# Sixteen-head attentions: normalising after a transpose to query rows, and adding the residual for four entries at once

## The chip, the cores and the metric

The kernel runs on one core of one Trainium2 chip. The metric is the device time of one execution, in microseconds (us). Before the change three executions took 15986.45, 16016.19 and 16036.29 us; the median is **16016.19 us**. The profiled execution has a span of 16008.8 us.

## What is computed

The reference is a decoder of four layers over 32 entries of 128 tokens with 128 features, in 32-bit floats. The state x is updated by twelve blocks in turn, each in the form

```
x = x + block(layernorm(x))
```

Five of the twelve blocks are attentions with 16 heads of 8 features, and they are what this change touches: L0 attention (causal), L0 cross attention, L1 attention, L1 cross attention (with a mask given as input) and L2 cross attention. For one entry they compute

```
q, k, v = projections of layernorm(x)   # cross attentions: k and v from a context of 128 tokens
scores  = q_h k_h^T / sqrt(8)           # for each head h, 128 x 128
attn    = softmax(scores)               # over the keys
out_h   = attn v_h                      # 128 x 8 for each head
x       = x + concat(out_h) Wo + bo     # L1 attention has no Wo; L0 attention has no bo
```

The softmax is computed as exp(scores) without taking off a maximum. Its denominator, the sum of the exponentials over the keys, is divided out after the product with v. Since no maximum is taken off, the kernel keeps the extremes of all reciprocals of these sums; if one lay out of bounds at the end, the whole program would be run again in a general form. With the inputs used here that second run does not happen.

## The kernel before

Class `Fast` holds the attention as `mha`, called once for each of the five blocks. It loops over 8 groups (`b4`) of 4 entries, 40 groups over the five blocks. The state X lies in SBUF for the whole program, with the 128 tokens of an entry on the 128 partitions.

**Head of a group.** `norm4` normalises four entries on VectorE (L333), `trans4` transposes them on TensorE (L341) into one PSUM tile and copies it to SBUF on VectorE (L343) as xnT. TensorE then makes q, k and v (through the helper `mm`, so that all these matmuls are recorded as L315). ScalarE and VectorE write q out as four masked copies `qTm` (L1385 to L1391), ScalarE writes kT and the values `va` (L1405). In `va` each head has its 8 value columns in one of four places of a row of 64, and eight columns of ones in the matching place of the second half.

**Loop over entries.** For each of four entries (`j2` and `jj`) TensorE makes the scores of 16 heads in PSUM tiles `sc`, transposed: keys on partitions, queries along the free dimension. In the causal block (L0 attention) and the one with a mask (L1 cross attention) a matmul with the tile `drop` comes first. ScalarE takes the exponential into `PT` (L1424). Then the matmuls `av` add up, for each head, its 8 outputs and eight copies of its sum. The PSUM tile `av` of two entries has queries along the free dimension; on partitions, for t = 0 and 1, it has 32 rows of outputs (four heads of 8) and 32 rows with the sums that belong to them.

**Normalising.** For two entries together VectorE takes, in four pieces of 32 partitions, the reciprocal of the sums (L1436, tile `rc`, 32x256) and multiplies the outputs with it (L1437, into `oT`). Since heads and features are on the partitions of `oT`, each sum has to be inverted eight times, once for each feature. `look` then reduces `rc` to its minimum and maximum (L1306).

**Projection and residual.** `oT[:, j, :]` has the layout that a matmul takes as stationary operand, so `y` of one entry is one matmul with Wo (in L1 attention one transpose, L1444), with a second one of one row for the bias in the cross attentions (`brow`). `addx` adds y to X (L347) and takes the statistics for the next layernorm (`stats`, L320 and L321), one entry at a time.

What sets the order: each engine works through its own queue. The order in these queues is chosen when the program is built, by a scheduler that takes ready instructions by their order in the source; the instructions wait for each other by semaphores. The buffers count too: all PSUM tiles made by `p1` (`p`, `av`, `y`) share four slots of one bank each, those made by `p2` (`sc`) two slots of two banks each. SBUF tiles of the loop (`wk`) have two slots each.

Of the kernel before, what the change touches and what calls it, by code (L numbers as in the profile page):

```python
# [13 lines left out]
F32 = mybir.dt.float32  # L14
# [4 lines left out]
ALU = mybir.AluOpType  # L19
# [1269 lines left out]
class Fast(General):  # L1289
# [38 lines left out]
    def mha(self, pre, cross, scale, causal=False, mask=None, out=True):  # L1328
        if self.general:
            return super().mha(pre, cross, scale, causal, mask, out)  # L1330
        nc, tc = self.nc, self.tc
        ob = f"{pre}_bo" in self.row_at
        with ExitStack() as es:
            wk = es.enter_context(tc.tile_pool(name=pre, bufs=2))
# [25 lines left out]
            if cross:  # L1360
# [12 lines left out]
            for b4 in range(NB // 4):  # L1373
                xnT = self.trans4(wk, self.norm4(wk, self.X, b4))
                kvT = self.ctxT[:, 512 * b4:512 * b4 + 512] if cross else xnT
                qp = self.p1([128, 512])
                self.mm(qp, self.mat(f"{pre}_q"), xnT)

                qTm = wk.tile([128, 4, 4, 128], F32, tag="qTm", name="qTm")
                for r in range(4):  # L1380
                    o = qTm[:, r].rearrange("p b q -> p (b q)")
                    m = self.sm("m4")[:, r:r + 1]
                    if r < 2:
                        if cross:
                            nc.scalar.activation(o, qp, AF.Identity, bias=qb[:, r:r + 1], scale=m)  # L1385
                        else:
                            nc.scalar.activation(o, qp, AF.Copy, scale=m)
                    elif cross:
                        nc.vector.tensor_scalar(o, qp, m, qb[:, r:r + 1], ALU.mult, ALU.add)
                    else:  # L1390
                        nc.vector.tensor_scalar(o, qp, m, None, ALU.mult)  # L1391
                kp = self.p1([128, 512])
                self.mm(kp, self.mat(f"{pre}_k"), kvT)
                kT = wk.tile([128, 512], F32, tag="kT", name="kT")
                if cross:
                    nc.scalar.activation(kT, kp, AF.Identity, bias=self.col(f"{pre}_bk"))
                else:
                    nc.scalar.copy(kT, kp)
                vp = self.p1([128, 512])
                for j in range(4):  # L1400
                    c = slice(128 * j, 128 * j + 128)
                    self.mm(vp[:, c], kvT[:, c], self.mat(f"{pre}_v"))
                va = va2[b4 % 2]
                diag = bass.AP(va.tensor, va.offset, [list(va.ap[0]), [256, 16], [72, 4], [1, 8]])
                nc.scalar.copy(diag, vp.rearrange("p (g r e) -> p g r e", g=16, r=4))  # L1405
                oT = wk.tile([128, 4, 128], F32, tag="oT", name="oT")
                rc = wk.tile([128, 4, 128], F32, tag="rc", name="rc")
                for j2 in range(2):

                    av = self.p1([128, 2, 2, 128], "av")  # L1410
                    for jj in range(2):
                        j = 2 * j2 + jj
                        c = slice(128 * j, 128 * j + 128)
                        PT = wk.tile([128, 16, 128], F32, tag="PT", name="PT")
                        for s in range(2):
                            sc = self.p2([128, 2, 512], "sc")
                            if drop is not None:
                                for u in range(2):
                                    self.mm(sc[:, u, :], self.identh[:, 0, :], drop.rearrange("p r q -> p (r q)"),
                                            stop=False)  # L1420
# [12 lines left out]
                    for s in range(2):  # L1433
                        for t in range(2):
                            g = 32 * (2 * s + t)
                            nc.vector.reciprocal(rc[g:g + 32, b2, :], av[64 * t + 32:64 * t + 64, s])  # L1436
                            nc.vector.tensor_tensor(oT[g:g + 32, b2, :], av[64 * t:64 * t + 32, s],  # L1437
                                                    rc[g:g + 32, b2, :], ALU.mult)
                self.look(rc)
                for j in range(4):  # L1440
                    b = 4 * b4 + j
                    y = self.p1([128, 128], "y")
                    if not out:
                        nc.tensor.transpose(y, oT[:, j, :], self.ident)  # L1444
                    else:
                        self.mm(y, oT[:, j, :], self.mat(f"{pre}_o"), stop=not cross)
                        if cross:
                            self.mm(y, self.ones, brow, start=False)
                    self.addx(b, y)


STAGES = ("l0_attn", "l0_xattn", "l0_ffn", "l1_attn", "l1_xattn", "l1_ffn", "l2_attn", "l2_xattn", "l2_ffn",
# [31 lines left out]
```

## Time and profile before

| what | value |
|---|---|
| TensorE (PE) busy | 9793.1 us, 61% of the span |
| VectorE (DVE) busy | 6850.5 us, 43% |
| ScalarE (ACT) busy | 3482.7 us, 22% |
| GpSimd (POOL) busy | 2735.0 us, 17% |
| reductions of L1306, 80 | 682 ns each |
| multiplies of L1437, 320 | 417 ns each |
| residual adds X<-X,y of L347 in the first 4160 us, 192 | 293 ns each |
| exponentials of L1424, 320 | 1022 ns each |
| mean clock granted to TensorE | 0.732 |

The five attentions lie in the first quarter of the span: 39 to 347, 347 to 705, 1345 to 1680, 1680 to 2012 and 3807 to 4156 us. The rest of the program (feed-forward blocks, other attentions and a six-layer local-attention stack that begins near 8600 us) does not call the changed function.

How to read the profile: a row of the groups has the line, the engine, the operation, the tiles as out<-in, the shapes (partitions x elements) and the count; then, after a bar, the busy time in us and the mean of one in ns; then the idle time of that engine just before, with what ended most of it. A row of the timeline has the start and the duration in us, then the same names, and in brackets the idle time before it and its releaser. PE is TensorE's matmul, PEld its load of the stationary operand. A 32-bit matmul is recorded as two passes, so one `y` is two rows in a count. A row of busy times by stretch gives the stretch, its length, the busy time (and instructions) of PE, PEld, DVE, ACT and POOL, then TensorE's granted clock as a share of full speed, the DMA share and GB/s.

### The profile page before, as it was taken

How to read it: one execution, taken by the hardware profiler on the slowest of the kernel's cores; microseconds unless marked ns; L12 is line 12 of the kernel's file. 1: busy time of each engine (PE TensorE's matmuls, PEld its weight loads, DVE VectorE, ACT ScalarE, POOL GpSimd, SP SyncE). 2: the span in 40 equal slices, each digit the busy share in tenths (PEclk: the TensorE clock that was granted, in tenths of full speed). 3: DMA queues.
4: the chain of work that ended last, by engine and by line, in shares of the span. 5: the costliest groups of instructions: out<-in, count | busy, mean ns of one | idle time of the engine just before them, and what ended most of it. 6: DMA issues, size and time to landing. Idle time of an engine off the chain costs nothing.

```text
span 16008.8 us, 131017 instructions
## 1 busy us (share of the span) xinstructions
PE 9793.1 (61%) x51289; PEld 6778.4 (42%) x51289; DVE 6850.5 (43%) x16132; ACT 3482.7 (22%) x4582; POOL 2735.0 (17%) x1578
## 2 busy tenths in 40 slices
PE   6676744447754444344445667667667667767667
PEld 3453333335433322233223445445445444544544
DVE  5545521124333333433334444444444444444444
ACT  2212200011101111111111333333333333333332
POOL 0000055530000000000000221221221221221221
PEclk8756856656666666666666888888888888888888
DMA  0000000001000010000100000000000000000000
GB/s 19 1 0 1 1 30 26 24 20 44 1 11 17 17 22 17 17 17 17 21 18 19 1 1 7 1 1 7 1 1 7 1 1 7 1 1 1 1 1 6
DMA packets 151407, 160.46 MB, mean 10 GB/s; under 512 B 18562, under 2 KB 130915, under 8 KB 145406
## 3 DMA queue, kind: packets, MB, share of 16 engines
q1 hardware_dynamic: 125340, 115.11, 3.3%
q0 software_dynamic: 24576, 33.60, 0.7%
q8 instruction: 410, 6.72, 0.2%
q10 hardware_dynamic: 866, 3.26, 0.1%
q14 instruction: 215, 1.76, 0.0%
HBM read 114.94 MB, written 36.96 MB: 9 GB/s over the span
## 4 chain that ended last, share of the span: by engine, by line
PE 34%; DVE 18%; POOL 7%; ACT 6%; DMA 4%; issue 2%; SPq 0%; ACTq 0%; POOLq 0%; DVEq 0%
PE av L315 6%; PE y L315 4%; PE op L315 4%; DMA rows<-scr 3%; DVE work L1050 3%; PE qk L315 3%; PE p L1200 3%; POOL raw L1183 3%; PE pt L1227 2%; DVE raw L1181 2%; DVE rt L1178 2%; POOL raw L1193 2%; DVE thr L1052 2%; PE sc L315 2%; PE tp L315 2%
## 5 line engine op out<-in xcount | busy, mean ns | idle before, releaser
L1183 POOL TENSOR_TENSOR raw<-raw,rt 128x1024 f32<-128x1024 f32 x384 | 902.2, 2349 | 5399.9 <-DVE raw L1181 5351.9
L315 PE MATMUL av<-va,PT 128*128 128x65 f32 x6144 | 1019.0, 318 | 346.8 <-ACT PT L1229 346.7
L315 PEld LDWEIGHTS av<-va,PT 128*128 128x128 f32 x6144 | 902.0, 226 | 662.9 <-ACT PT L1229 662.9
L315 PE MATMUL tp<-mix,ex 128*128 128x128 f32 (+1 forms) x2048 | 302.0, 315 | 1358.5 <-POOL ex L1063 1358.5
L315 PE MATMUL qk<-wqkv,zs 128*128 128x512 f32 x1536 | 847.4, 669 | 439.8 <-DVE raw L1181 269.6
L1200 PE MATMUL p<-ident,raw 128*128 128x128 f32 x3072 | 525.9, 344 | 597.2 <-POOL raw L1193 597.2
L315 PEld LDWEIGHTS tp<-mix,ex 128*128 128x128 f32 (+1 forms) x2048 | 254.2, 173 | 1401.4 <-POOL ex L1063 1362.9
L1436 DVE RECIPROCAL rc<-av 32x256 f32<-32x256 f32 x320 | 561.9, 1756 | 521.1 <-PE av L315 517.8
L1200 PEld LDWEIGHTS p<-ident,raw 128*128 128x128 f32 x3072 | 480.5, 183 | 669.5 <-POOL raw L1193 669.5
L1178 DVE TENSOR_TENSOR rt<-qk,tab 128x512 f32<-128x512 f32 x768 | 498.6, 686 | 555.4 <-ACT sq L1174 290.6
L1193 POOL TENSOR_TENSOR raw<-raw,ss 128x2048 f32<-128x2048 f32 x192 | 690.7, 3618 | 118.2 <-DVE ss L564 118.2
L1234 DVE RECIPROCAL rs<-av 128x4 f32<-128x4 f32 x768 | 140.3, 183 | 1327.1 <-PE av L315 1327.1
L1229 ACT COPY PT<-pt 128x512 f32<-128x512 f32 x768 | 449.9, 586 | 941.5 <-PE pt L1227 941.5
L315 PE MATMUL mp<-rows,mix 128*128 128x512 f32 (+1 forms) x320 | 191.9, 766 | 733.9 <-DMA rows<-scr 733.9
L1174 ACT ACTIVATE sq<-qk 128x1024 f32<-128x1024 f32 x384 | 393.3, 1024 | 1130.6 <-DVE ss L1184 756.3
L315 PE MATMUL vp<-wqkv,zs 128*128 128x512 f32 x768 | 418.6, 672 | 330.4 <-DVE t L1222 167.8
L1227 PE MATMUL pt<-ident,t 128*128 128x128 f32 x3072 | 536.6, 303 | 137.2 <-ACT t L1223 137.2
L315 PEld LDWEIGHTS qk<-wqkv,zs 128*128 128x128 f32 x1536 | 273.4, 203 | 731.1 <-issue 579.6
L1201 DVE COPY qkT<-p 128x512 f32<-128x512 f32 x384 | 265.6, 692 | 716.7 <-PE p L1200 716.7
L1059 POOL TENSOR_TENSOR ex<-ex,e 128x1188 f32<-128x1188 f32 x32 | 85.9, 2683 | 2762.6 <-DVE e L1058 2697.7
L605 POOL DMA_INDIRECT gd<-in_tdn,idx x512 | 483.1, 943 | 432.0 <-DVE idx L598 181.7
L1223 ACT ACTIVATE t<-t 128x1024 f32<-128x1024 f32 x384 | 407.8, 1062 | 650.9 <-DVE t L1222 650.2
(364 smaller groups left out, 20372.4 us busy)
## 6 DMA issues: line engine op xcount, KB each, us to landing
scr<-dots SPq DMA_DIRECT2D x32, 1056.0 KB
rows<-scr SPq DMA_DIRECT2D x512, 66.0 KB
T<-flt SPq DMA_DIRECT2D x16, 1024.0 KB
wqkv<-in_dqkv SPq DMA_DIRECT2D x6, 1536.0 KB
gd<-in_tdn,idx POOLq DMA_INDIRECT x512
gt<-in_tup,idx POOLq DMA_INDIRECT x256
wo<-in_dwo SPq DMA_DIRECT2D x6, 512.0 KB
X<-in_x SPq DMA_DIRECT2D x4, 512.0 KB
```

What stands on the lines that cost most here:

```text
L315: self.nc.tensor.matmul(out, lhsT=lhsT, rhs=rhs, start=start, stop=stop)
L605: self.nc.gpsimd.indirect_dma_start(out=out, out_offset=None, in_=table, in_offset=bass.IndirectOffsetOnAxis(ap=idx, axis=0))
L1050: nc.vector.match_replace(out=work[:, 0:n], in_to_replace=m8, in_values=cur, imm_value=-3.4e38)
L1174: nc.scalar.activation(sq, pp, AF.Square)
L1178: nc.vector.tensor_tensor(t[:, :, o:o + 32], pp[:, :, n:n + 32], tab[:, w, 1, o:o + 32].unsqueeze(1).to_broadcast([128, 16, 32]), ALU.mult)
L1183: nc.gpsimd.tensor_tensor(r, r, t, ALU.add)
L1193: nc.gpsimd.tensor_tensor(raw, raw, rn.unsqueeze(2).to_broadcast([128, 32, 64]), ALU.mult)
L1200: nc.tensor.transpose(p[:, c, :], flat[:, o:o + 128], self.ident)
L1223: nc.scalar.activation(t, t, AF.Exp, scale=8.0)
L1227: nc.tensor.transpose(pt[:, c, :], t[:, 4 * e + c, :], self.ident)
L1229: nc.scalar.copy(PT, pt)
L1436: nc.vector.reciprocal(rc[g:g + 32, b2, :], av[64 * t + 32:64 * t + 64, s])
```

## The change

The normalising is moved to the other side of a transpose. ScalarE copies `av` of two entries out of PSUM into `avs`; four transposes on TensorE bring it to query rows (`tp`: queries on 128 partitions, outputs and sums along the free dimension). There a sum is needed once for a head and a query, so VectorE's reciprocal covers 32 elements on 128 partitions (two entries of 16 heads), and the multiply, with the reciprocal broadcast over the eight features, 256 elements on 128 partitions. The result `ao` has query rows, so that L1 attention, which has no projection, can add it to X as it is; the others transpose it back with `trans4` (four transposes and a copy on VectorE) for the projection. The tile `y` holds all four entries in one PSUM bank, and one add of 128x512 takes the place of four of 128x128; the statistics are taken after it. `look` reduces 64 elements in place of 512.

```diff
--- before.py
+++ after.py
@@ -1403,8 +1403,8 @@
                 va = va2[b4 % 2]
                 diag = bass.AP(va.tensor, va.offset, [list(va.ap[0]), [256, 16], [72, 4], [1, 8]])
                 nc.scalar.copy(diag, vp.rearrange("p (g r e) -> p g r e", g=16, r=4))
-                oT = wk.tile([128, 4, 128], F32, tag="oT", name="oT")
-                rc = wk.tile([128, 4, 128], F32, tag="rc", name="rc")
+                ao = wk.tile([128, 4, 16, 8], F32, tag="ao", name="ao")
+                rc = wk.tile([128, 4, 4, 4], F32, tag="rc", name="rc")
                 for j2 in range(2):
 
                     av = self.p1([128, 2, 2, 128], "av")
@@ -1429,24 +1429,34 @@
                                     h = 4 * (2 * s + t) + r
                                     self.mm(av[64 * t:64 * t + 64, s, jj, :], va[:, j, h, :], PT[:, h, :],
                                             start=r == 0, stop=r == 3)
+                    avs = wk.tile([128, 2, 2, 128], F32, tag="avs", name="avs")
+                    nc.scalar.copy(avs, av)
+
+                    tp = self.p1([128, 2, 2, 2, 2, 4, 8], "tp")
+                    for jj in range(2):
+                        for s in range(2):
+                            nc.tensor.transpose(tp[:, jj, s].rearrange("p t w r e -> p (t w r e)"), avs[:, s, jj, :],
+                                                self.ident)
+                    tv = tp.rearrange("p j s t w r e -> p (j s t) w r e")
                     b2 = slice(2 * j2, 2 * j2 + 2)
-                    for s in range(2):
-                        for t in range(2):
-                            g = 32 * (2 * s + t)
-                            nc.vector.reciprocal(rc[g:g + 32, b2, :], av[64 * t + 32:64 * t + 64, s])
-                            nc.vector.tensor_tensor(oT[g:g + 32, b2, :], av[64 * t:64 * t + 32, s],
-                                                    rc[g:g + 32, b2, :], ALU.mult)
-                self.look(rc)
-                for j in range(4):
-                    b = 4 * b4 + j
-                    y = self.p1([128, 128], "y")
-                    if not out:
-                        nc.tensor.transpose(y, oT[:, j, :], self.ident)
-                    else:
-                        self.mm(y, oT[:, j, :], self.mat(f"{pre}_o"), stop=not cross)
+                    rv = rc[:, b2].rearrange("p j g r -> p (j g) r")
+                    nc.vector.reciprocal(rv, tv[:, :, 1, :, 0])
+                    nc.vector.tensor_tensor(ao[:, b2].rearrange("p j (g r) e -> p (j g) r e", g=4), tv[:, :, 0],
+                                            rv.unsqueeze(3).to_broadcast([128, 8, 4, 8]), ALU.mult)
+                self.look(rc.rearrange("p j g r -> p j (g r)"))
+                if out:
+                    oT = self.trans4(wk, ao.rearrange("p j h e -> p j (h e)"), "oT")
+                    y = self.p1([128, 4, 128], "y")
+                    for j in range(4):
+                        self.mm(y[:, j, :], oT[:, 128 * j:128 * j + 128], self.mat(f"{pre}_o"), stop=not cross)
                         if cross:
-                            self.mm(y, self.ones, brow, start=False)
-                    self.addx(b, y)
+                            self.mm(y[:, j, :], self.ones, brow, start=False)
+                else:
+                    y = ao.rearrange("p j h e -> p j (h e)")
+                x = self.X[:, 4 * b4:4 * b4 + 4, :]
+                nc.vector.tensor_tensor(x, x, y, ALU.add)
+                for j in range(4):
+                    self.stats(x[:, j, :], 4 * b4 + j)
 
 
 STAGES = ("l0_attn", "l0_xattn", "l0_ffn", "l1_attn", "l1_xattn", "l1_ffn", "l2_attn", "l2_xattn", "l2_ffn",
```

More of the change, by code (lines that the diff above doesn't have):

```diff
@@ L1439, in mha @@
-                self.look(rc)
-                for j in range(4):
-                    b = 4 * b4 + j
-                    y = self.p1([128, 128], "y")
-                    if not out:
-                        nc.tensor.transpose(y, oT[:, j, :], self.ident)
-                    else:
-                        self.mm(y, oT[:, j, :], self.mat(f"{pre}_o"), stop=not cross)
-                        if cross:
-                            self.mm(y, self.ones, brow, start=False)
-                    self.addx(b, y)
+                    avs = wk.tile([128, 2, 2, 128], F32, tag="avs", name="avs")
@@ new lines, in mha @@
+                    rv = rc[:, b2].rearrange("p j g r -> p (j g) r")
[8 more added lines that the diff above has]
+                        self.mm(y[:, j, :], oT[:, 128 * j:128 * j + 128], self.mat(f"{pre}_o"), stop=not cross)
+                        if cross:
+                            self.mm(y[:, j, :], self.ones, brow, start=False)
+                else:
+                    y = ao.rearrange("p j h e -> p j (h e)")
```

## Prediction

> **What bounds the kernel now.** I read the page first, then the groups of VectorE by line, then the timeline over one group of four entries in each of the five attentions, and last the busy times of single groups. Of the 16008.8 us the five attentions hold the stretches 39 to 347, 347 to 705, 1345 to 1680, 1680 to 2012 and 3807 to 4156 us, 1682 us in all (the five windows' sum); the change can act only there. The page shows the row that it removes:
>
> ```profile
> L1436 DVE RECIPROCAL rc<-av 32x256 f32<-32x256 f32 x320 | 561.9, 1756 | 521.1 <-PE av L315 517.8
> ```
>
> The mean of one is 1756 ns, and there are eight in each of the 40 groups. What counts is where they lie. The timeline of the sixth group of the L0 cross attention:
>
> ```profile
> 603.08 1.09 PE L315 MATMUL av<-PT,va 128*64 128x128 f32 x16
> ...
> 604.22 1.75 DVE L1436 RECIPROCAL rc<-av 32x256 f32<-32x256 f32 x1 [1.61 <-PE av L315]
> ...
> 606.63 1.76 DVE L1436 RECIPROCAL rc<-av 32x256 f32<-32x256 f32 x1
> ...
> 609.18 1.75 DVE L1436 RECIPROCAL rc<-av 32x256 f32<-32x256 f32 x1
> ...
> 611.92 1.76 DVE L1436 RECIPROCAL rc<-av 32x256 f32<-32x256 f32 x1
> ...
> 614.52 0.50 PEld L315 LDWEIGHTS y<-mats,oT 128*128 128x128 f32 x2 [9.29 <-DVE oT L1437]
> 614.52 0.80 PE L315 MATMUL y<-mats,oT 128*128 128x128 f32 x2 [9.10 <-DVE oT L1437]
> ...
> 617.41 0.71 PEld L341 LDWEIGHTS p<-ident,xn 128*128 128x128 f32 x4 [0.22 <-issue]
> ```
>
> The last av matmuls end at 604.17. TensorE's next work but for the tail of entry 0's and 1's projections is at 614.52, 10.35 us later, and the next group's first transposes (617.41) stand behind the projections. The four reciprocals of the second pair of entries lie wholly on that path; those of the first pair (593.73 to 602.6) lie beside the scores of entries 2 and 3 and cost nothing. So a group is a chain: head (transposes, q, k, v) 7.3 us, loop over four entries (scores 582.80 to av's end 604.17) 21.4, wait 10.35, projections 2.9: 41.9 us, the spacing of the undisturbed groups.
>
> The busy times of two such groups show a second limit, TensorE's clock (the column behind POOL):
>
> ```profile
> 478.50:527.70 49.20, 35.44 (x194) 20.75 (x192) 24.82 (x39) 10.47 (x12) 0.00 (x0) 0.60 0.00 1
> 573.20:615.10 41.90, 27.09 (x193) 15.96 (x192) 24.76 (x39) 10.47 (x12) 0.00 (x0) 0.79 0.00 1
> ```
>
> Same instructions, 0.60 instead of 0.79, 7.3 us longer. Within a group q/k matmuls of the head take about 0.85 us, and the projections are spaced 0.73 us apart after the wait but 0.42 us inside the loop: the wait puts TensorE at half clock, and the head pays.
>
> **What the Trainium skill says.** "TensorE: Matmul & The Clock Gate", section "Part 1: The HAM clock gate (the "warmup" mystery)", says that the clock is halved after an idle window of about 3.4 us and restored after a busy one; the trace agrees in kind (10 us of wait, then 0.73 for 0.42 us). The same page, "Part 4: PE-mode transpose", says that transposes do not count as busy in the same way; the trace before does not separate this, so I count the new transposes as no help for the clock. "VectorE: DVE Perf Modes", section "Why `tensor_reduce` can't reduce along partition axis", says that the engine streams along the free dimension and that each partition is a lane of its own, so 32 rows should cost what 128 do. The trace agrees: L1437's multiply of 32x256 takes 417 ns, L1235's of 128x256 takes 424.
>
> **The change, part by part.** Per group of four entries.
>
> VectorE loses 8 reciprocals x 1756 = 14.0 us and 8 multiplies x 417 = 3.3. It gets 2 reciprocals of 128x32 (353 ns, L326's row of just that shape) and 2 multiplies of 128x256 (424): 1.6 us. The two reductions of L1306 go from 512 elements (682 ns) to 64; those of L1313 and L1314, of 40 elements, take 162 and 187, so I estimate 215 each. Four residual adds of 0.29 become one of 128x512, about 0.68 (L658, same shape, one input in PSUM); the statistics stay. With an output projection, one copy of 128x512 comes in (0.69, L343). VectorE falls from 24.8 to about 9 us per group and is no bound at all.
>
> ScalarE gets 2 copies of 128x512 out of PSUM, 0.585 each (L1405). It is busy 10.5 of 41.9 us, so the sum costs nothing; the second copy is on the path.
>
> TensorE gets 8 transposes of av, and 4 of ao with a projection; 4 transposes go in l1_attn. Four in a row take 1.06 to 1.11 us after a wait (L341); warm I estimate 0.85 (0.21 between starts in L1261's runs, plus the end). The first pair's four add 0.85 us to the loop; entries 0 and 1's projections, two in L0a and two with bias in the cross attentions, leave it, but only one of them (0.42) stood between av matmuls.
>
> The new path from the end of av to the projection: semaphore 0.2, copy 0.58, 0.2, transposes 0.85, 0.2, reciprocal 0.35, multiply 0.47, 0.2, transposes of ao 1.0, 0.2, copy 0.66, 0.2: **5.1 us in place of 9.7 to 10.35**. The two reductions run beside the second transposes. The 0.2 is what stands between an end and a dependent start on another engine (0.21 before L347 and L343). But now all four projections are behind it: with bias eight pairs of passes at 0.73 = 5.8 us against 2.9; without bias four at 0.5 = 2.0 against 1.0.
>
> The next group's transposes were always behind the last y (617.41 after 616.69), and y still takes its PSUM slot first, so I keep that order. Queued behind them on VectorE: the joined add (0.68) and up to eight statistics operations (4 x 0.47) can stand before the copy of xnT, for which q, k and v wait. In before the add was 0.29 and the copy came at once. I charge 0.8 us with a projection, 2.6 us in l1_attn, where no projection lies between.
>
> Sums at the clock of now: l0_attn loop 20.9 - 0.42 + 0.85 = 21.3, path 5.1, y 2.0, head 6.85 + 0.8: 36.0 against 38.4, 2.4 saved. Cross: 21.4 + 0.43 + 5.1 + 5.8 + 8.1 = 40.8 against 41.9, 1.1 saved; the masked one is 40.2 against 41.3, the same. l1_attn: loop 21.2 - 0.3 + 0.85 = 21.75, copy and transposes 1.9, head 7.3 + 2.6 = 9.9: 33.5 against 38.7, 5.2 saved. Eight groups each: (2.4 + 3 x 1.1 + 5.2) x 8 = **87 us**.
>
> The clock: the wait without TensorE work shrinks from 10 us to three gaps of about 1 us. It will still fall to half somewhere in them, but the 5.8 us of projections and the transposes after them then run without a gap, so it should be back by q, k and v. In the cross attentions the last third of the projections (8 x 0.31 saved at most = 2.5; I take 1.0) and most of four q/k passes at 0.85 and the v passes (about 4.5 us at half; I take 2.0 saved): 3.0. l0_attn has 2.0 us of projections: 0.8. l1_attn has two gaps of about 1 us and less: 1.2. Together (3 x 3.0 + 0.8 + 1.2) x 8 = **88 us**. Forecast 16016 - 175 = **15841 us**.
>
> **Rivals.** (a) The clock stays as now: the chain shrinks, the half clock covers tail and head alike. For it: the path holds transposes and one short burst. 16016 - 87 = 15929. (b) More than forecast: also the disturbed loops disappear. Mean spacing of groups is 44.2, 41.7 and 43.8 us in l0_xattn, l1_attn and l2_xattn against 41.9, 38.7 and 41.9 undisturbed: (2.3 + 3.0 + 1.9) x 8 = 58 us; and without the charge for the queue (0.8 x 4 + 2.6) x 8 = 46: 15737. Against it: these drops come in the middle of the loop (L1a, 1531 to 1545 us), where the change adds little. (c) A new wait eats it: the first pair's transposes wait for ScalarE's copy, which stands behind two exponentials (1.94 us together), with all later scores queued behind them on TensorE. Twice per group, 80 x 1.94 = 155 us: 15996, no change. Against it: av ended at 593.7, the exponentials began at 594.83, so the copy (0.58) fits ahead of them. (d) Slower: transposes in the loop lower TensorE's activity, and the three attentions without mask matmuls run their loops at half clock. The group at 0.60 took 49.2; 24 groups going from a mean of 43.2 to 48.2 cost 120 us, and at a clock of 0.5, by the same slope (7.3 us per 0.19), 3.8 us more each, 211 in all; less 87: 16049 to 16140, middle 16095. For it: these loops already drop by themselves. Against it: 0.85 us of transposes in 21 us is little.
>
> **How the numbers follow.** Forecast 0.45, (a) 0.25, (b) 0.15, (c) 0.08, (d) 0.07. The bound of 0.3% is 48 us: faster below 15968, slower above 16064. Forecast, (a) and (b) are faster, 0.85; (c) and a part of (d) no change, 0.09; the rest slower, 0.06. The range goes from a little below (b) to just past (a), 15700 to 15970, which leaves out (c), (d) and the tail of (b).
>
> **What would show it.** Right, if the reciprocal's row shrinks to 80 of about 353 ns, TensorE's wait before the projections splits into three of about 1 us, and the head's q/k passes fall from 0.85 toward 0.5 us. Rival (a) if they stay at 0.85; (c) if the transposes of av wait on ScalarE in the loop; (d) if groups in l0_xattn show a clock near 0.6. Wrong altogether if the next group's transposes move ahead of the projections: then the path is hidden too, and the time falls below 15700. Work outside the five attentions should keep its time; should it not, the forecast fails for a reason not treated here.

## The result, and the profile after

Four executions of the changed kernel took 15756.74 to 15808.76 us, median **15768.08 us**, against 16016.68 us for the kernel before on the same chip: ratio **0.9851, 95% interval 0.9828 to 0.9874**. The forecast was 15841 us. The profiled spans are 16008.8 and 15754.9 us.

The time went where the prediction looked for it. From the first `rstd` to the last residual add of each attention, read from the two traces:

| attention | before, us | after, us | gained | forecast | spacing of groups before | after |
|---|---|---|---|---|---|---|
| L0 self (causal) | 317.0 | 273.5 | 43.5 | 25.6 | 38.6 | 32.8 |
| L0 cross | 355.3 | 309.0 | 46.3 | 32.8 | 44.5 | 38.5 |
| L1 self | 336.8 | 268.3 | 68.5 | 51.2 | 41.0 | 31.5 |
| L1 cross (masked) | 334.2 | 306.9 | 27.3 | 32.8 | 41.4 | 37.7 |
| L2 cross | 351.7 | 300.1 | 51.6 | 32.8 | 44.0 | 37.2 |

The five sum to 237 us; the rest of the program took 14313.8 us before and 14297.2 after. "Spacing" is the mean of the seven distances between the first writes of `qTm` of successive groups.

The page and the groups by shape of the changed kernel, as they answer to the reciprocal's row of before:

```profile
PE 9835.9 (62%) x51705; PEld 6797.8 (43%) x51705; DVE 6166.0 (39%) x15564; ACT 3530.6 (22%) x4662; POOL 2735.4 (17%) x1578
L1443 DVE RECIPROCAL rc<-tp 128x32 f32<-128x32 f32 x80 | 32.4, 405 | 902.7 <-PE tp L1438 902.7
```

The reciprocals fell from 561.9 us to 32.4. Their median is 358 ns, as the prediction took; one took 2321 ns and lifts the mean to 405. VectorE as a whole lost 684 us, and the program only 254: most of VectorE's work had lain beside other work.

The same place in the timeline as shown of before, in the second half of a group of the L0 cross attention:

```profile
527.21 0.59 ACT L1433 COPY avs<-av 128x512 f32<-128x512 f32 x1 [1.19 <-PE av L315]
527.85 0.66 PE L1438 MATMUL tp<-ident,avs 128*128 128x128 f32 x4 [0.69 <-ACT avs L1433]
528.34 0.38 PE L341 MATMUL p<-ident,ao 128*128 128x128 f32 x2
528.54 0.36 DVE L1443 RECIPROCAL rc<-tp 128x32 f32<-128x32 f32 x1 [8.91 <-PE tp L1438]
528.94 0.42 DVE L1444 TENSOR_TENSOR ao<-tp,rc 128x256 f32<-128x256 f32 x1
...
529.42 0.44 PE L341 MATMUL p<-ident,ao 128*128 128x128 f32 x2 [0.69 <-DVE ao L1444]
529.89 0.69 DVE L343 COPY oT<-p 128x512 f32<-128x512 f32 x1 [0.28 <-PE p L341]
530.64 0.80 PE L315 MATMUL y<-mats,oT 128*128 128x128 f32 x2 [0.78 <-DVE oT L343]
531.37 0.79 PE L315 MATMUL y<-brow,ones 1*128 1x128 f32 x2
...
536.43 1.11 PE L341 MATMUL p<-ident,xn 128*128 128x128 f32 x4
536.53 0.69 DVE L1457 TENSOR_TENSOR X<-X,y 128x512 f32<-128x512 f32 x1 [5.95 <-PE y L315]
537.58 0.69 DVE L343 COPY xnT<-p 128x512 f32<-128x512 f32 x1 [0.36 <-PE p L341]
...
538.32 2.08 PE L315 MATMUL p<-xnT,mats 128*128 128x512 f32 x2 [0.78 <-DVE xnT L343]
```

TensorE's one wait of 10.35 us is now three of 0.69, 0.69 and 0.78 us, 3.47 us with the work between them. Behind it the four projections run without a gap for 5.79 us. And yet the pairs of passes in them start 0.73 us apart (530.64 to 531.37), as before behind the long wait, and the two passes for q that follow take 2.08 us, where in the L0 self attention the four for q and k together take 1.98 (from 202.47).

The busy times of these stretches show it (after the busy counts: the clock). First the path, the projections with bias and the head in the L0 cross attention; then the same three in the L0 self attention; then one loop over four entries in each:

```profile
527.17:530.64 3.47, 1.31 (x9) 0.84 (x9) 1.72 (x5) 0.59 (x1) 0.00 (x0) 0.94 0.00 0
530.64:536.43 5.79, 5.79 (x17) 4.00 (x17) 0.00 (x0) 0.00 (x0) 0.00 (x0) 0.50 0.00 0
536.43:543.75 7.32, 6.54 (x18) 3.85 (x17) 4.03 (x12) 2.13 (x3) 0.00 (x0) 0.50 0.00 0
...
196.46:199.93 3.47, 2.00 (x12) 0.98 (x11) 1.73 (x5) 0.59 (x1) 0.00 (x0) 1.00 0.00 0
199.93:200.93 1.00, 1.00 (x9) 1.00 (x9) 0.00 (x0) 0.00 (x0) 0.00 (x0) 1.00 0.00 0
200.93:206.49 5.56, 3.47 (x18) 2.12 (x17) 4.76 (x16) 2.33 (x4) 0.00 (x0) 1.00 0.00 0
...
543.75:564.71 20.96, 17.45 (x165) 9.67 (x164) 0.78 (x2) 9.03 (x10) 0.00 (x0) 1.00 0.00 1
174.05:196.46 22.41, 21.25 (x178) 10.71 (x179) 0.78 (x2) 8.67 (x9) 0.00 (x0) 1.00 0.00 1
```

In the cross attention everything behind the path runs at 0.50, although TensorE is busy for 12.33 of these 13.11 us. In the self attention, which has no bias, the clock stays full. The last two rows are used below: with mask matmuls (174.05) TensorE is busy 0.95 of the loop, without (543.75) 0.83, and the loop with them is 1.45 us longer.

For comparison the last projections (two of four) and the head before the change, in the group that the prediction shows:

```profile
614.52:617.41 2.89, 2.89 (x8) 2.00 (x8) 2.11 (x6) 0.00 (x0) 0.00 (x0) 0.50 0.00 0
617.41:624.70 7.29, 6.32 (x21) 3.69 (x22) 2.99 (x6) 2.40 (x4) 0.00 (x0) 0.56 0.00 0
```

The head takes 7.32 us where it took 7.29: in the cross attention the shorter wait has not brought the clock back. The clock records change at steps of 3.41 us. In the group of the changed kernel they are at half from 530.25 to 543.90 us, four steps. This is the second of them:

```profile
533.66:537.08 3.42, 3.42 (x11) 2.52 (x12) 0.55 (x1) 0.00 (x0) 0.00 (x0) 0.50 0.00 0
```

TensorE was never idle in it, with projections and bias passes, and the clock stayed at half after it.

### The profile page after: what moved, and what is told of

Its sections match the earlier page's. It is cut to its first block, busy times and chain, and to the rows that moved or that the text cites. A ratio compares the mean times of both kernels' runs of the same rounds, so it can differ in the third digit from the quotient of the medians.

```text
span 15754.9 us, 131362 instructions
## 1 busy us (share of the span) xinstructions
PE 9835.9 (62%) x51705; PEld 6797.8 (43%) x51705; DVE 6166.0 (39%) x15564; ACT 3530.6 (22%) x4662; POOL 2735.4 (17%) x1578
## 3 DMA queue, kind: packets, MB, share of 16 engines
q10 hardware_dynamic: 866, 3.26, 0.1%
## 4 chain that ended last, share of the span: by engine, by line
PE 35%; DVE 19%; POOL 7%; ACT 6%; DMA 4%; issue 2%; SPq 0%; ACTq 0%; POOLq 0%; DVEq 0%
PE av L315 6%; PE y L315 4%; PE op L315 4%; DMA rows<-scr 3%; DVE work L1050 3%; PE qk L315 3%; PE p L1200 3%; POOL raw L1183 3%; PE pt L1227 2%; DVE raw L1181 2%; DVE rt L1178 2%; POOL raw L1193 2%; DVE thr L1052 2%; PE sc L315 2%; PE tp L315 2%
## 5 line engine op out<-in xcount | busy, mean ns | idle before, releaser
L315 PE MATMUL sc<-qTm,kT 32*128 32x512 f32 x1536 | 511.7, 717 | 77.4 <-DVE P L518 63.3
```

The lines of the kernel that those rows point to most:

```text
L315: self.nc.tensor.matmul(out, lhsT=lhsT, rhs=rhs, start=start, stop=stop)
```

## The experiments

Twelve kernels ran, in four sets. Each set has its own runs of the kernel before, on its own chip; the kernel before differs by up to 1% between chips, so only ratios are compared. A block is an attention from its first `rstd` to its last residual add. Mean spacing of groups, from the traces (us):

| kernel | ratio, 95% | L0 self | L0 cross | L1 self | L1 cross | L2 cross |
|---|---|---|---|---|---|---|
| before | 1 | 38.6 | 44.5 | 41.0 | 41.4 | 44.0 |
| the change | 0.9851 (0.9828–0.9874) | 32.8 | 38.5 | 31.5 | 37.7 | 37.2 |
| e1_norm | 0.9861 (0.9845–0.9878) | 34.5 | 38.4 | 30.9 | 37.4 | 39.8 |
| e2_resid | 1.0055 (1.0038–1.0072) | 36.3 | 45.7 | 42.2 | 37.8 | 45.7 |
| e2b_nohoist | 0.9999 (0.9990–1.0008) | 39.5 | 43.5 | 40.9 | 41.3 | 43.2 |
| e3_nobias | 0.9855 (0.9835–0.9874) | 33.0 | 36.9 | 31.5 | 33.7 | 40.6 |
| e4_hold_before | 1.0002 (0.9993–1.0011) | 38.6 | 43.1 | 39.9 | 41.2 | 43.7 |
| e4c_hold36 | 0.9976 (0.9964–0.9988) | 38.7 | 42.0 | 39.9 | 39.3 | 42.7 |
| e5_biasfirst | 0.9870 (0.9852–0.9887) | 33.3 | 37.8 | 31.5 | 31.6 | 41.9 |
| e7_zeromask | 0.9857 (0.9839–0.9875) | 33.4 | 37.3 | 31.5 | 37.5 | 37.7 |
| e10_zero_bias | 0.9779 (0.9762–0.9797) | 33.5 | 31.8 | 31.5 | 31.6 | 31.6 |
| e12_fullrow | 0.9886 (0.9869–0.9902) | 32.8 | 42.3 | 33.2 | 36.6 | 38.3 |
| e13_fullrow_zero | 0.9837 (0.9821–0.9853) | 32.6 | 36.6 | 31.5 | 36.6 | 37.0 |
| e11_pipe_zero_bias | 0.9743 (0.9726–0.9759) | 28.9 | 30.7 | 26.2 | 29.9 | 30.4 |

### Which half of the change carries the gain

**The normalising alone** (`e1_norm`): the changed kernel with a projection tile and an add for each entry, as before.

```diff
-                    y = self.p1([128, 4, 128], "y")
-                    ...
-                nc.vector.tensor_tensor(x, x, y, ALU.add)
+                    y = self.p1([128, 128], "y")
+                    self.mm(y, oT[:, 128 * j:128 * j + 128], self.mat(f"{pre}_o"), stop=not cross)
+                    ...
+                    self.addx(b, y)
```

> The normalising on query rows alone; projections, residual adds and statistics stay one entry at a time, as before. Theory 1 (the shorter path from av to the projections, and the clock that follows from it, are the whole gain): about 15770 us, within 40 us of the changed kernel, and next group's transposes still behind the four projections. Rival 2 (the joined y tile and the single add carry a good part of it): 15850 us or more.

0.9861 against 0.9851: the intervals overlap, as theory 1 has it, so the normalising carries all that can be measured.

**The joined residual alone** (`e2_resid`): the kernel before with `y` of four entries in one tile and one add.

```diff
-                    y = self.p1([128, 128], "y")
...
-                    self.addx(b, y)
+                y = self.p1([128, 4, 128], "y")
...
+                x = self.X[:, 4 * b4:4 * b4 + 4, :]
+                nc.vector.tensor_tensor(x, x, y, ALU.add)
```

> The joined y tile and the single residual add alone, on top of the kernel before; the reciprocals stay on 32 rows. By the prediction's own steps it can only lose: the projections of entries 0 and 1 wait with the others, (1.0 + 3 x 2.9 + 0.3) x 8 = 80 us, so about 16095 us. Rival 3 (one y tile takes one PSUM slot instead of four, so the next group's transposes, q, k and v no longer stand behind the projections of entries 2 and 3 and fill the 10 us wait): up to 7.3 us for each of 35 group boundaries, 255 us, so 15760 to 15900 us; q and k matmuls would then lie between the reciprocals in the trace.

It costs 0.55% (77 us between the medians). That this is close to the 80 us of the first theory is luck: the projections of entries 0 and 1 do not wait (in the group below they start at 513.97 and 515.82 us, before the wait). Rival 3 had the new order right and its effect wrong. With one PSUM slot for four projections in place of four, the next group's transposes, q, k and v move ahead of the projections of entries 2 and 3. The timeline of a group of the L0 cross attention in this kernel shows what that does:

```profile
517.35 0.69 DVE L343 COPY xnT<-p 128x512 f32<-128x512 f32 x1
...
521.08 1.75 DVE L1436 RECIPROCAL rc<-av 32x256 f32<-32x256 f32 x1
...
522.87 0.81 DVE L1389 TENSOR_SCALAR qTm<-p,c_small,qb 128x512 f32<-128x512 f32 x1
...
524.12 1.76 DVE L1436 RECIPROCAL rc<-av 32x256 f32<-32x256 f32 x1
525.92 0.81 DVE L1389 TENSOR_SCALAR qTm<-p,c_small,qb 128x512 f32<-128x512 f32 x1
...
526.78 2.07 PE L315 MATMUL sc<-qTm,kT 32*128 32x512 f32 x2 [3.21 <-DVE qTm L1389]
...
528.78 0.80 PE L315 MATMUL y<-mats,oT 128*128 128x128 f32 x2
```

The head now lies in the wait, but its writes of `qTm` stand between reciprocals of 1.75 us in VectorE's queue, so the next scores wait 3.21 us for them. That alone is not the loss. The two attentions with mask matmuls became shorter with the same reciprocals in the queue, L0 self from 317.0 to 311.7 us and L1 cross from 334.2 to 318.6. The three without became 26 to 30 us longer each, and there the time at half clock grew, in the L0 cross block from 185 to 279 us.

**The same without the new order** (`e2b_nohoist`): `e2_resid` with three one-column matmuls that take the PSUM slots that the four tiles took, so the order stays that of before.

```diff
+                    if j:
+                        d = self.p1([128, 1], "d")
+                        self.mm(d, oT[:, j, :], self.ident[:, 0:1])
```

> The same as the residual part alone, but entries 1, 2 and 3 each also take a PSUM slot for a matmul of one column whose result nobody reads, so that four slots are taken in a group as before. Rival 3: the next group's transposes are behind the projections again and the gain of the residual part is gone, 16000 to 16100 us. If the gain were VectorE's (one add in place of four), this kernel would be as fast as the residual part alone.

0.9999: with the order kept the loss is gone. The single add is worth nothing here; what cost was the head moved ahead, in the three attentions whose loops then ran at half clock.

### Is it the path or the clock

**Without bias** (`e3_nobias`): the changed kernel without the bias matmuls in the three cross attentions, which leaves the bias out.

```diff
-                        if cross:
-                            self.mm(y[:, j, :], self.ones, brow, start=False)
```

> The changed kernel with the bias of the output projection left out in the three cross attentions (four one-row matmuls per group). Theory 4 (TensorE falls to half clock there because the projections with their one-row bias matmuls keep it too little occupied): the clock stays full from group to group as in L0 attention, a cross group goes from 37.5 to about 30.5 us, 24 groups, 168 us: about 15600 us. Rival 5 (the clock falls in the gaps of the path from av to the projections, whatever follows): only the time of the bias matmuls goes, 3.8 us per group, 91 us: about 15675 us, and the clock of a cross group stays near 0.8.

Neither number came: 0.9855, where the change has 0.9851. The masked attention gained (37.7 to 33.7), but groups of the other two lay at 30 to 33 or at 41 to 48: many lost inside the loop, at half clock, what they had gained on the path. This gave the next theory: a loop without mask matmuls lies at the edge of what keeps the clock up.

**Clock held, chain unchanged** (`e4_hold_before`, `e4c_hold36`): the kernel before with unread matmuls in its wait, 24 and then 36.

```diff
+                    if j == 2:
+                        hd = self.p2([128, 2, 512], "hd")
+                        for n in range(24):
+                            self.mm(hd[:, n % 2, :], self.identh[:, 0, :], self.half[:, 0:512])
```

> The kernel before, with 24 products of half-precision matrices that nobody reads put on TensorE into its 10 us wait of each group (after the projections of entries 0 and 1, ahead of those of 2 and 3). The wait for the reciprocals stays as long as it is. Theory A (half of what the change won is the clock, as the prediction's sum has it: 87 us chain, 88 us clock): projections and the head's q/k passes come at full clock (q/k 0.43 instead of 0.85 us apart), groups of a cross attention shorten from 41.9 by about 5 us with an undisturbed loop; 5 blocks together 100 to 200 us less: ratio 0.988 to 0.994. Rival B (the chain alone counts, the clock does not follow from the wait): groups as before, ratio 0.999 to 1.001.

> As the run with 24 unread products, with 36: there the products ended after 4.9 us (0.21 us each) and TensorE still stood idle for 3.6 us, after which the clock fell as before. 36 last about 7.7 us at full clock and leave about 1 us of the 8.8 us wait. Theory A (the wait itself halves the clock for projections and head): now the clock stays full in the attentions' tails; head and projections shorten by 4 to 5 us in the three cross attentions and by 2 to 3 in the two others where the loop is undisturbed: 100 to 180 us less, ratio 0.989 to 0.994. Rival B (the chain alone counts): 0.999 to 1.001. Where the products start at half clock they take up to 15 us and lengthen the group: then a ratio above 1.

24 were too few: they ended after 4.9 us, 3.6 us of idle time were left, and the clock fell as before. With 36 the clock holds where the loop was undisturbed. Stretches of filler, second half of the projections, and head in a group of the L1 cross attention with 36:

```profile
1769.07:1778.24 9.17, 8.81 (x41) 3.84 (x41) 8.85 (x14) 0.00 (x0) 0.00 (x0) 1.00 0.00 0
1778.24:1779.90 1.66, 1.66 (x8) 1.18 (x8) 1.63 (x4) 0.00 (x0) 0.00 (x0) 1.00 0.00 0
1779.90:1785.73 5.83, 3.54 (x18) 2.18 (x17) 3.96 (x13) 2.50 (x4) 0.00 (x0) 1.00 0.00 0
```

Projections 1.66 us for the 2.89 of the half clock, head 5.83 for 7.29 (these two from the rows of the L0 cross attention before): 2.7 us, the 38.7 against 41.4 of most of its groups. Over the program 0.24%, 38 us: the rival's zero is out, and theory A had it too large. L1 self went from 41.0 to 39.9 with 24 as with 36; 2.4 us of idle time were left there. One group of L0 self grew to 44.4.

The clock records of the five blocks add up to 738 us at half clock before, 312 with 36 unread matmuls and 423 with the change. So 425 us less at half clock brought 38 us (part of them had lain in the wait, where they cost nothing), and the change, which left more at half clock, brought 237. The clock matters, but the change's gain is mostly the shorter chain.

**Bias ahead, and zero masks** (`e5_biasfirst`, `e7_zeromask`, `e10_zero_bias`): the changed kernel with the bias added by one matmul of 512 columns ahead of the projections; with mask matmuls of zeros in the attentions that have no mask; with both.

```diff
+                        self.mm(y.rearrange("p j d -> p (j d)"), self.ones, brow4.rearrange("p j d -> p (j d)"),
+                                stop=False)
...
-                        if cross:
-                            self.mm(y[:, j, :], self.ones, brow, start=False)
```

```diff
-            if causal or mask is not None:
-                drop = one.tile([128, 4, 128], BF16, name="drop")
+            drop = one.tile([128, 4, 128], BF16, name="drop")
+            if not causal and mask is None:
+                nc.gpsimd.memset(drop, 0.0)
```

> The changed kernel, with the bias of the three cross attentions added by one matmul of one row and 512 columns ahead of the four projections, in place of one of 128 columns after each. Theory 5 (the bias passes stand on the path behind the wait at half clock, about 0.72 us each): groups of the cross attentions shorten by 4 to 5 us, 24 x 4.5 = 108 us: ratio to before 0.978. Theory 6 (loops without mask matmuls lie at the edge of activity at which the clock is halved, and what the path gains is lost again in such loops, as without any bias): the masked L1 cross attention shortens by about 4 us a group (30 us), L0 and L2 cross not: ratio 0.983 to 0.986, with loops at half clock in those two.

> The changed kernel, with mask matmuls of zeros also in the three attentions that have no mask (L0 cross, L1 self, L2 cross); they run while TensorE waits for ScalarE's exponentials. Theory 6: these loops stay at full clock as those of the masked attentions do: L1 self falls from 31.5 to about 28.5 us a group (24 us in all), the cross groups go to the 37.7 of the masked L1 cross attention, from 38.4 and 37.2 (0 to 6 us): ratio to before 0.983 to 0.984. Rival (the mask matmuls cost their own time, 16 more passes an entry): these three attentions get 3 to 6 us a group longer, 70 to 140 us: ratio 0.990 to 0.994.

> The two former edits together on the changed kernel: bias in one matmul ahead of the projections, and mask matmuls of zeros where there is no mask. Theory 6: now the gain on the path is kept in all three cross attentions: groups at 33 to 34 us from 37.5, 24 x 4 = 96 us, and 20 us in L1 self: ratio to before 0.977 to 0.979. Rival (the groups fall into step with the clock's windows whatever is on the path, and each stays at 37.5): ratio 0.983 to 0.985.

Alone each is worth nothing (0.9870 and 0.9857 against 0.9851); together they take off another 0.7%, as theory 6 had it. With the bias ahead alone the masked attention goes to 31.6, and the unmasked ones have groups of 46.9. With zeros alone all cross attentions stand at about 37.5, the masked one's number, but L1 self, expected at 28.5, stays at 31.5: it has one slow group (36.7) in place of two (37.8 and 38.3), and the others grow, from 27.7–30.0 us to 29.9–31.6. Together all three cross attentions go to 31.6 to 31.8. The stretches of path, projections and head in the L0 cross attention with both:

```profile
435.41:439.18 3.77, 3.26 (x18) 1.72 (x18) 1.78 (x6) 0.58 (x1) 0.00 (x0) 1.00 0.00 0
439.18:440.17 0.99, 0.99 (x8) 0.99 (x9) 0.99 (x3) 0.00 (x0) 0.00 (x0) 1.00 0.00 0
440.17:444.39 4.22, 2.78 (x14) 1.66 (x13) 3.85 (x14) 2.50 (x4) 0.00 (x0) 1.00 0.00 0
```

TensorE is now busy 3.26 of 3.77 us on the path: the bias pass and the next group's transposes fill its gaps. Projections and head take 5.2 us in place of 13.1.

### Why the projections did not bring the clock back

**Bias of 128 rows** (`e12_fullrow`, `e13_fullrow_zero`): the changed kernel with the same number of bias passes at the same places, but over 128 rows, 127 of them zero; then with zero masks too.

```diff
-                            self.mm(y[:, j, :], self.ones, brow, start=False)
+                            self.mm(y[:, j, :], on128, brow128, start=False)
```

> The changed kernel, with each bias matmul of the cross attentions given 128 rows (weights of ones, a moving matrix with the bias in its first row and zeros below) in place of one row: the same number of passes at the same places. Theory 7 (one-row passes hardly count as activity, and so the 5.8 us of projections with bias don't bring the clock back, as the prediction expected of them): the clock is back within one or two of its windows, the head's q/k passes come 0.43 us apart, and the masked L1 cross groups fall from 37.7 to 33.5 to 34.5 us; L0 and L2 cross keep a part of it only, since their loops fall by themselves: ratio 0.979 to 0.983. Rival 8 (passes of 128 columns with a weight load each don't count as activity, whatever their rows): groups at 37.5 as now, ratio 0.984 to 0.986.

> The changed kernel with zero mask matmuls in the three attentions without a mask, as in the run of ratio 0.9857, and with the bias matmuls of 128 rows, still one after each projection, as in the run of ratio 0.9886. Theory 7 with the loops held busy (one-row passes don't count as activity; loops without mask matmuls lose the clock by themselves): both parts together keep the clock full in all three cross attentions, groups at 33.5 us as in the three clean groups of the L1 cross attention, from 37.5: 24 x 4 = 96 us less than the zero masks alone: ratio 0.979 to 0.981. Rival (what helped in the version with one bias matmul was that it left the path, and not the clock; eight pairs of passes behind the wait keep the groups at 37): ratio 0.984 to 0.989.

In a clean group of the masked L1 cross attention, 33.5 us long, projections and head in `e12_fullrow`; below them in `e1_norm`, where the projections too run at full clock, but the bias has one row:

```profile
1603.14:1605.03 1.89, 1.89 (x17) 1.89 (x17) 0.00 (x0) 0.00 (x0) 0.00 (x0) 1.00 0.00 0
1605.03:1610.89 5.86, 3.47 (x18) 2.11 (x17) 4.87 (x16) 2.50 (x4) 0.00 (x0) 1.00 0.00 0
```

```profile
1637.01:1640.33 3.32, 3.32 (x16) 2.35 (x16) 1.68 (x8) 0.00 (x0) 0.00 (x0) 1.00 0.00 0
1640.33:1647.50 7.17, 6.39 (x21) 3.80 (x20) 3.93 (x12) 2.13 (x3) 0.00 (x0) 0.52 0.00 0
```

At the same full clock one-row passes between the projections make them 3.32 us long, 128-row passes 1.89. (`e1_norm` has four `y` tiles; with the joined tile, in `e7_zeromask`, the same sixteen passes take 3.33 us from 379.16.) And after 3.32 us in which TensorE was never idle, the clock fell.

Two steps just before a fall in `e7_zeromask`; then one just before a fall in `e13_fullrow_zero`, and one with projections at half clock there, after which the clock was full:

```profile
379.25:382.66 3.41, 3.41 (x18) 2.44 (x19) 0.07 (x1) 0.00 (x0) 0.00 (x0) 1.00 0.00 0
413.39:416.80 3.41, 1.94 (x11) 1.13 (x9) 1.72 (x5) 0.00 (x0) 0.00 (x0) 1.00 0.02 5
```

```profile
415.01:418.42 3.41, 1.44 (x11) 0.45 (x9) 1.53 (x2) 1.53 (x4) 0.00 (x0) 1.00 0.00 0
449.14:452.55 3.41, 3.41 (x18) 3.20 (x16) 0.62 (x1) 0.00 (x0) 0.00 (x0) 0.50 0.00 0
```

In the three cross blocks of `e7_zeromask` the clock fell 24 times: 13 times after a step in which TensorE was at most 0.57 busy, 11 times after one of 0.77 to 1.00. The first row (379.25, all busy) is one of the 11; its work is projections and one-row passes. If the time of the one-row passes is left out, the 11 come to 0.48 to 0.60. With 128-row passes it fell 26 times, never after a step more than 0.57 busy. In `e10_zero_bias` it fell 7 times. So two things halve the clock here: a step that holds the gaps of the path or of the head's end, and a step full of one-row passes.

What the prediction needed is the way back. After a fall that followed a step 0.57 busy, in the gaps of the path, the clock stayed at half for three steps in ten of eleven cases of `e7_zeromask` (four in the other), and for one step in all ten of `e13_fullrow_zero`. The rows show the pair: 3.42 us of projections with one-row passes, wholly busy, leave the clock at half (533.66, in the result's section), and 3.41 us of the same projections with 128-row passes bring it back (449.14). So it was the one-row passes that kept the change's projections from restoring the clock.

That is worth little by itself. `e12_fullrow` gave 0.9886, outside both of its ranges, and `e13_fullrow_zero` 0.9837 for the expected 0.979 to 0.981, with 33.5 in the good groups and 35 to 41 in the others; its interval overlaps that of the zero masks alone (0.9857). The time at half clock in the three cross blocks was 211 us for 218: falls at the head's end came in place of the others and left the loop at half clock for two to four steps. One of these steps (425.25 to 428.66) was wholly busy with scores and mask matmuls, so one-row passes are not the only work that does not bring the clock back at once. Which groups lose the clock seems to depend on how they lie against the steps; that was not tried. In `e12_fullrow` the unmasked loops fell too, after steps of 0.66; other steps of 0.55 to 0.66 did not lead to a fall, so the busy share alone does not set the edge, and what else does stays open.

### A version that does better

`e11_pipe_zero_bias`: `e10_zero_bias` with the next group's head emitted between the two pairs of entries.

```diff
-            for b4 in range(NB // 4):
+            def head(b4):
...
+                return qTm, kT, va
...
+                    if j2 and b4 + 1 < NB // 4:
+                        nxt = head(b4 + 1)
```

> The version with bias in one matmul and zero masks (ratio 0.978), with the next group's norm transposes, q, k and v emitted between the first and second pair of entries, so that its scores can start in the tail of this group. Theory 9 (hoisting failed in the joined residual alone only because copies stood between reciprocals of 1.76 us on VectorE; with VectorE nearly free it pays): groups from 31.5 to 26 to 28 us, 40 x 4.5 = 180 us: ratio 0.965 to 0.970. Rival 10 (the head's passes take the place of scores in the loop, which is bound by TensorE's order and ScalarE's exponentials, and the tail is only shifted): groups at 30.5 to 32, ratio 0.976 to 0.980.

0.9743, the best of all, between the two theories: groups of 30.3 us with a projection and 27.7 without, in the steady part. One group of each kind:

```profile
460.00:490.30 30.30, 30.30 (x216) 15.78 (x214) 6.54 (x19) 11.86 (x14) 0.00 (x0) 1.00 0.00 1
1300.00:1327.70 27.70, 27.70 (x204) 14.10 (x202) 6.67 (x22) 11.68 (x14) 0.00 (x0) 1.00 0.01 1
```

TensorE is busy in all of these stretches at full clock: the tail is filled, and TensorE's own work is the bound. Not all groups are like that: 8 of the 21 distances in the cross attentions are 33.5 to 35.1 us, and eleven times in these blocks the clock fell after a step wholly busy with the bias pass of one row and 512 columns for about 1 us of it. A bias of 128 rows was not tried here.

The head moved ahead cost 0.55% in `e2_resid` and gains 0.4% over `e10_zero_bias` here. Two things differ, VectorE's queue and the masks that hold the loops' clock. In `e2_resid` the masked blocks gained although the queue was full, so that the queue decides, as theory 9 has it, is not shown.

## Why the prediction was right, and where it was not

The sign, the place and the main mechanism hold: the second pair's reciprocals were the path, and most of the gain is that path made shorter. The size is right in part by luck, since two errors cancel in the cross attentions. The measured time lies 73 us below the forecast and 31 above rival (b). By its own terms, for an undisturbed group of an L0 cross attention and one of L0 self:

| term | L0 cross: forecast | measured | L0 self: forecast | measured |
|---|---|---|---|---|
| loop | 21.8 | 20.96 | 21.3 | 22.41 |
| end of av to projection | 5.1 | 3.47 | 5.1 | 3.47 |
| four projections | 5.8 | 5.79 | 2.0 | 1.00 |
| head with queue charge | 8.1 | 7.32 | 7.65 | 5.56 |
| clock | −3.0 | 0 | −0.8 | in the rows above |
| sum | 37.8 | 37.5 | 35.2 | 32.4 |

- **The new path** was sized 1.6 us too long. The larger part is in the hops from engine to engine: each of the six was set at 0.2 us and is 0.03 to 0.06 in this timeline, 0.9 us less in all. The transposes of the first pair's outputs need no wait, so two of the four transposes of `ao` run at 528.34 beside the normalising, and the four of `av` took 0.66 us for the 0.85 that was set.
- **The four projections behind the wait** with bias came out as computed, 5.79 us.
- **The queue charge** was set too high: the copy of xnT goes directly behind the joined add (536.53, 537.58), and the statistics come after it. In the cross attention it waited 0.36 us, for TensorE. In L1 self, 2.6 us were charged; there only the add of 0.68 us stands ahead, and the next group's transposes run early, beside the normalising. Two of its groups, with a mean clock of 0.96 and 0.92, took 28.6 and 30.0 us, where 32.3 were forecast.
- **Clock back by q, k and v** is the step that failed, in the three cross attentions: 3.0 x 3 x 8 = 72 of the 88 us. The projections were to restore it; with one-row passes among them they don't: the clock stayed at half through all 13.1 us of projections and head, and in `e7_zeromask` for three steps after such a fall, where 128-row passes bring it back after one (`e13_fullrow_zero`). For the term of 3.0 us a group an undisturbed cross group got nothing. In L0 self, without bias, the clock gain was larger than set: the records show full clock without a break for 249 us, and projections and head take 6.6 us where 8.85 was forecast with the clock's share taken off (a part of this is the queue charge of 0.8).
- **The first pair's transposes** lengthen the loop by about 0.4 us in the cross attention (its exponentials start 5.79 us apart there, at 518.29 and 524.08, and 5.4 us from entry to entry before), where the projections that left it give back more, and bring the loop of the masked L0 self to 22.41 us, 1.1 more than was set. Rival (c) is out: the copy of `av` at 517.18 goes ahead of the exponentials, and the transposes follow 0.94 us after its start.
- **Rival (b)** was half true: no queue charge, and the mean spacing of L0 and L2 cross came nearer to the undisturbed one. In L1 self two of seven groups still took 37.8 and 38.3 us, at a clock of 0.68. The two errors (a path sized too long, a clock gain that did not come) cancel in the cross groups, 37.8 against 37.5; what remained beyond the forecast is in L0 self, L1 self and the disturbed loops.
- **Rival (d)** did not come with the change itself, but its danger is real: in `e3_nobias`, `e5_biasfirst` and `e12_fullrow` unmasked groups of 41 to 48 us ate what the edit had gained elsewhere, or more.
- The prediction wrote that transposes of the next group moving ahead of the projections would hide the path and bring the time below 15700. `e2_resid` shows the opposite in the kernel before. In the changed one they move ahead in `e5_biasfirst` too, and its unmasked attentions lose; in `e10_zero_bias`, with masks in every loop, the time does fall below 15700 (15650 us). It depends on whether the loops keep their clock.

The Trainium skill, "TensorE: Matmul & The Clock Gate", section "Part 1: The HAM clock gate (the "warmup" mystery)", speaks of an idle window that halves the clock and a busy one that restores it, and gives the window as 3413 ns. The steps of 3.41 us in these records agree. The rule does not suffice here: the clock fell after steps 0.57 busy and after one that was wholly busy with one-row passes in it (379.25), and a wholly busy step did not restore it (533.66).

## What to carry to other kernels

Cut the chain behind the last wait first, and ask of each instruction in it how many elements each lane has and whether it repeats a value: the reciprocal cost 1756 ns for 256 elements a lane and 358 for 32. Then look at the clock by stretch before crediting a shorter wait with a faster clock, since work that fills TensorE need not count as work: here a one-row bias in a tail kept it at half. Moving work of the next group into a wait can lose time if the loop behind it then runs at half clock: in `e2_resid` it cost the unmasked attentions 26 to 30 us each and gained 5 and 16 in the masked ones. And two edits that each bring nothing (the bias ahead, a zero mask) may bring 0.7% together.

## What was not expected of the hardware

- One-row passes alternating with 128-row passes are slow by themselves: eight passes of each kind took 3.32 us at full clock, and 1.89 us when all had 128 rows.
- Mask matmuls of zeros hold the clock in a loop that waits for ScalarE, at a price: a loop with masks is 1.45 us longer (22.41 against 20.96), yet the three unmasked blocks together had 188 us at half clock with zeros and 324 without, and the L1 self block fell from 268.3 to 261.2 us. Over the program, added alone, they bring nothing that can be measured (0.9857 against 0.9851).
- Groups can fall into step with the clock's windows: the undisturbed L0 and L2 cross groups of the changed kernel, and most L0 self groups of `e4c_hold36`, are 37.5 us long, eleven steps of 3.41 us. Whether the step is the cause was not tried.
